# Two graph layers on one core: sums over seen edges go to layer 2's accumulators through DRAM; products of the list use five PSUM banks, additions three bunches behind

## The chip, the cores and the metric

The kernel runs on one core of a Trainium2 chip. The core has five engines with queues of their own: PE (TensorE, matmuls; PEld is its loading of weights), DVE (VectorE), ACT (ScalarE), POOL (GpSimd) and SP (SyncE, which here only issues DMAs). Each works through its instructions in order and waits on semaphores where an instruction needs another engine's or a DMA's result. The metric is device microseconds (us) of one execution, and the median of several runs is compared.

## The reference

A relational graph network of two layers over N = 12,500 nodes of 128 features and 200,000 edges, sorted by their target node. An edge's relation is the greatest of ten of its attributes. In each layer a node takes, for each of ten relations, the mean of its neighbours' features, multiplies it with that relation's matrix, and adds its own features times a root matrix and a bias. The first layer ends in a relu; behind the second come the residual and a layer norm.

```python
def _rgcn_layer(x, src, dst, edge_type, w_rel, root, bias):
    seg = dst * NUM_REL + edge_type
    sums = jax.ops.segment_sum(x[src], seg, num_segments=N * NUM_REL)
    cnt = jax.ops.segment_sum(jnp.ones(seg.shape, x.dtype), seg, num_segments=N * NUM_REL)
    mean = (sums / jnp.maximum(cnt, 1.0)[:, None]).reshape(N, NUM_REL, -1)
    return jnp.einsum('nrd,rdo->no', mean, w_rel) + x @ root + bias
...
edge_type = jnp.argmax(msg[:, NODE_EMB_DIM:-NODE_EMB_DIM], axis=1).astype(jnp.int32)
h = jax.nn.relu(_rgcn_layer(x, src, dst, edge_type, w_rel1, root1, b1))
return _rgcn_layer(h, src, dst, edge_type, w_rel2, root2, b2)      # then _layernorm(x + ...)
```

## The kernel before

**Tiles of edges.** The edges lie in 1,563 tiles of 128. For a tile GpSimd gathers the 128 source rows from DRAM with one indirect DMA (`gathered`, L751) into a buffer `g`; DVE makes a one-hot matrix `oh` of the edges' (relation, node) places (`ones`, L765 in layer 1 and L768 for the list of layer 2); ACT multiplies it with the edges' weights, one over the count (`weighted`, L757); PE multiplies both into a PSUM bank `zp` (L978 in layer 1, L1480 in layer 2); and DVE adds `zp` to the accumulators (`sum_into`, L792) at a place that it reads from a register. In the profile each of these float matmuls counts as two records.

**Accumulators.** `cc` holds two rings in SBUF, one for each layer, of 10 relations x (1,024 nodes + 120 columns beyond the end). The nodes go through a ring in blocks, mostly of 256, so that a lap has four. When a block has all its edges, `folded` (at the start of a lap, L729) adds what lies beyond the end; `projected` (L739, ten matmuls with the relations' matrices, and L742 one for the root) makes the block's output; and the place is cleared by ACT (`cleared`, L722) in two halves for the next lap. The place of an addition is known only as a range of nodes when the program is built. A range that lies across the end of a lap is declared as the whole ring (`offsets`), so that an addition there is ordered behind everything that is still under way in the ring.

**Layer 1** (`layer_1`) walks over all 1,563 tiles. The first 166 gather rows of x (512 B). The other 1,397 gather rows of 1 KB, x and h side by side, from tables in which the h of finished nodes has been written: an edge whose source is finished when the walk comes by is a *seen* edge, and its h row goes to layer 2's ring (ring 1) with the same one-hot, in the same addition (`ALL`). When a block k is done, `finish` issues its projection, and sets for some tiles later (`todo.at`, where u is four tiles): the activation and transposes (`rows_out`), the stores of h by SP (`rows_kept`), `second`, which projects ring 1 with layer 2's matrices and adds root 2 x h, `second_kept`, which adds the bias and stores the result to `T2` in DRAM on SP's queue, and the clears of both rings. `second` and its clears stand for blocks of seen edges (`both`).

**Layer 2** (`layer_2`) has the edges that were not seen. It gathers from `hD`, the h rows in DRAM: first 166 tiles as they were, in the meantime DVE and PE bring the unseen edges together into a list (`brought_together`), then 695 tiles of that list. Two walks share the rings: walk 0 (the low nodes) sums into ring 1, walk 1 into ring 0. The work is cut into bunches, each as many products as one PSUM bank holds. A bunch's one-hots are made four bunches ahead (`AH`) and its additions stand two bunches behind (`BE`); `zp` has three banks (`ps_y`), one more is `ps_m`'s, for the making of the list. There are seven gather buffers `g` of eight tiles and six one-hot buffers (`OB`). A list tile may be wider than 48 places and is then multiplied in column pieces, each with a one-hot table of its own (`tables[(c, WZ)]`). When a block is done, `finish` projects it, adds `T2` through an identity matmul (L742), and sets `turn` (ACT, transposes), `norm` (`normed`, L700 to L710, then the store of the output) and two `cleared` at 8u and 12u.

**Order.** Nothing is left to a planner: each engine's order is that in which the program emits its instructions, and the due times above set it. A queue that waits holds all that stands behind it.

Of the kernel before, what the change touches and what calls it, by code (L numbers as in the profile page):

```python
# [32 lines left out]
OB = 6  # L33
# [31 lines left out]
def rgcn_resnorm_kernel(ctx: ExitStack, tc: tile.TileContext, x, src, dst, attr, w_rel1, root1, b1,  # L65
# [145 lines left out]
    T2 = dram.tile([C, N], F32, name="T2")  # L211
# [426 lines left out]
    def rows_in(k):  # L638

        last = "e" if k == len(ranges[-1]) - 1 else ""  # L640
        xb = fin.tile([P, len(block(k)[2]) if last else 4, C], F32, name="xb" + last)
        rows_dma(xb, x, k, False)
        return xb

    def features_in(k, l, xb):

        n0, n, subs = block(k)
        last = "e" if k == len(ranges[-1]) - 1 else ""
        fT = fin.tile([P, (len(subs) if last else 4) * P], F32, name="fT" + last)
# [17 lines left out]
    def shifted(po, k, l):  # L667

        n = block(k)[1]
        tail = {NBLK - 1: "e", NBLK - 2: "d"}.get(k, "")  # L670
        a = fin.tile([P, P if tail else YB], F32, name="a" + tail)
        nc.scalar.activation(a[:, :n], po[:, :n], AF.Identity if l else AF.Relu, bias=bsb[l])  # L672
        return a
# [19 lines left out]
    def normed(k, xb, pr):  # L693

        v = fin.tile([P, 4, C], F32, name="v")
# [12 lines left out]
        o = fin.tile([P, 4, C], F32, name="o")  # L708
        for t, h in subs:
            nc.vector.tensor_scalar(o[:h, t, :], v[:h, t, :], mv[:h, t, 0:1], rstd[:h, t:t + 1],  # L710
                                    op0=ALU.subtract, op1=ALU.mult)
        rows_dma(o, out, k, True)
# [19 lines left out]
    def projected(k, l, last, po=None, more=True, ring=None):  # L732

        n0, n, _ = block(k)
        o = n0 % RN
        if po is None:
            po = ps_f.tile([P, YB], F32, name="pf")
        for r in range(NREL if more else 0):
            nc.tensor.matmul(po[:, :n], wsb[l][:, r, :], cc[:, l if ring is None else ring, r, o:o + n],  # L739
                             start=(r == 0), stop=False)  # L740
        w, f = last
        nc.tensor.matmul(po[:, :n], w, f[:, :n], start=not more, stop=True)  # L742
        return po
# [15 lines left out]
    def ones(keys, cols, n, w):  # L759

        oh = dpool.tile([P, YB], F32, name="oh")
        m = NREL * w
        o = oh[:, :n * m]
        if w == WN:
            nc.vector.tensor_tensor(o.rearrange("p (t m) -> p t m", m=m), cols[:, None, :m].to_broadcast([P, n, m]),  # L765
                                    keys[:, :, None].to_broadcast([P, n, m]), op=ALU.is_equal)
        else:
            nc.vector.tensor_tensor(o.rearrange("p (t r n) -> p t r n", r=NREL, n=w),  # L768
                                    cols[:, None, :, :w].to_broadcast([P, n, NREL, w]),
                                    keys[:, :, None, None].to_broadcast([P, n, NREL, w]), op=ALU.is_equal)  # L770
        return oh
# [60 lines left out]
    def layer_1():  # L832
# [6 lines left out]
        def finish(k, t):  # L839
# [8 lines left out]
            po = [projected(k, 0, (rsb[0], fTs[k]))]  # L848
# [4 lines left out]
            def rows_out(_):  # L853
                a = po.pop()
                a = fin_a.setdefault(k, shifted(a, k, 0))
                pr = ps_f.tile([P, 4, C], F32, name="pf")
                n0, n, subs = block(k)
# [33 lines left out]
            if k < NBLK - 1:  # L891
                todo.at(t + (9 if k >= NBLK - 3 else 3) * u, second)
                todo.at(t + (9 if k >= NBLK - 3 else 4) * u, second_kept)
            else:
                todo.run(t)
                todo.run(END)
                todo.at(t, second)
                todo.at(t, second_kept)
# [4 lines left out]
            if k + 1 < NBLK - 1:  # L903
# [10 lines left out]
                def turned_kept(t):  # L914
                    n0, n, subs = block(k + 1)
                    pt = po.pop()
                    fTs[k + 1] = fin.tile([P, 4 * P], F32, name="fT")
# [6 lines left out]
        fin_a = {}  # L924
# [117 lines left out]
    ps_m = fast.enter_context(tc.tile_pool(name="ps_m", bufs=1, space=PSUM))  # L1042
    ps_y = fast.enter_context(tc.tile_pool(name="ps_y", bufs=3, space=PSUM))
    idxB = comp.tile([P, NT2], I32, name="idxB")
# [13 lines left out]
    def brought_together(ready, first):  # L1058
# [15 lines left out]
        for to, a, o in ((Si, src, 0), (A[:, P:], CN, 0), (K, KD, L)):  # L1074
# [3 lines left out]
            if whole < NR:  # L1078
                nc.sync.dma_start(to[whole:NR, :real], bass.AP(a.tensor, a.offset + o + (NT - RT) * P, [[ER, 1], [1, real]]))
        tri, wide = flat[:, at:at + P], flat[:, at + P:at + P + NREL * WZ].rearrange("p (r n) -> p r n", n=WZ)  # L1080
        assert at + P + NREL * WZ <= NREL * RW
        yield 1
        nc.vector.tensor_tensor(wide, spread[:, :, None].to_broadcast([P, NREL, WZ]),
                                columns[:, None, :WZ].to_broadcast([P, NREL, WZ]), op=ALU.add)
# [85 lines left out]
        for c in range(0, WMAX, WZ):  # L1170
            w = min(WZ, WMAX - c)
            t = mask[:, c * NREL:(c + w) * NREL].bitcast(F32).rearrange("p (r n) -> p r n", n=w)
            nc.vector.tensor_scalar(t, wide[:, :, :w], float(c), None, op0=ALU.add)
            tables[c, WZ] = t
        assert WMAX * NREL <= ER
# [5 lines left out]
        def put(i, c):  # L1181
# [5 lines left out]
            o = WMAX * NREL + i * (EW // P)  # L1187
# [101 lines left out]
    def layer_2():  # L1289
# [90 lines left out]
        def fetched(k):  # L1380
# [4 lines left out]
            if k != partial:  # L1385
                assert k != final or partial in ended
                xbs[k] = (comp if tail else fin).tile([P, 4, C], F32, name="xb" + tail)
                rows_dma(xbs[k], x, k, False)
            fTs[k] = (comp if tail else fin).tile([P, 4 * P], F32, name="fT" + tail)
            nc.sync.dma_start(fTs[k][:, :n], T2[:, n0:n0 + n])  # L1390

        def finish(k, i):
# [8 lines left out]
            po = [projected(k, 1, (ident, fTs[k]), ring=ring)]  # L1401
# [10 lines left out]
            def turn(_):  # L1412
                a = fin.tile([P, YB], F32, name="a")
                nc.scalar.activation(a[:, :n], po.pop()[:, :n], AF.Copy)
                if k == partial:
                    nc.sync.dma_start(T2[:, n0:n0 + n], a[:, :n])
                    fetched(following[0])
                    return
                pr = ps_f.tile([P, 4, C], F32, name="pf")
# [25 lines left out]
        AH, BE = 4, 2  # L1445
# [5 lines left out]
        for p in range(-AH, NB + BE):  # L1451
            if p + AH < NB:
# [3 lines left out]
                ohs[p + AH] = ones(keys[:, t0:t0 + n], tables[(c, WZ) if second else WN], n, w)  # L1456
# [6 lines left out]
            if p < 0:  # L1463
                continue
            if p < NB:
# [23 lines left out]
            q = p - BE  # L1489
            if q >= 0:  # L1490
                l, second, t0, n, w, c, whole = bunches[q]
                assert not l or "ring" in ready
                for j in range(n):
                    t = t0 + j
                    if (second, t) not in offs:
# [4 lines left out]
                        else:  # L1500
                            m = min(GB2, T0 - t)
                            if t % CT == 0:
                                row = rows_.tile([1, CT], I32, name="row")
                                nc.scalar.dma_start(row, b_i[t // CT:t // CT + 1, :])
                            vals = offsets(row[:, t % CT:t % CT + m], t, m, bounds)
# [184 lines left out]
```

## Time and profile before

| | us |
|---|---|
| median of the runs (3112.14 to 3119.51) | 3114.19 |
| the profiled execution | 3108.35 |
| its span, first to last instruction | 3106.5 |
| PE busy | 2368.2 |
| PEld busy | 1949.5 |
| DVE busy | 2031.1 |
| ACT busy | 1301.6 |
| POOL busy | 2295.8 |

The mean granted TensorE clock was 0.84 of full speed. Layer 1's gathers run from 4 to 1,958 us, layer 2's from 1,969 to 3,052 us. DMA moved 370.97 MB. A row of the costliest groups has a line, an engine, an operation, out<-in, a count, then busy time and the mean of one in ns, then the idle time of the engine ahead of them and what ended most of it. A row of the waits has the waiting line, what it waited for, microseconds in total, times, and the longest. A row of a timeline has the start, the duration, the instruction, and in brackets the idle time before it and what ended that.

### The profile page before, as it was taken

Reading aid. Unit: us, or ns where it says so; the run is one execution under the profiler, and the core shown is the slowest. Engines: PE = TensorE matmul, PEld = TensorE weight load, DVE = VectorE, ACT = ScalarE, POOL = GpSimd, SP = SyncE. Lnnn points to the kernel's source line nnn. Section 1 sums busy time; section 2 is a strip of 40 time slices with the busy share of each in tenths; the row PEclk is TensorE's granted clock in tenths of the full one; section 3 lists DMA queues with packets and bytes.
Section 4 is the critical chain, followed back from the end, with each engine's and each line's share of the span. In section 5 each row is a group of like instructions: output and inputs, shape, how many; then the busy total and the mean of one; then the engine's idle time right before and its main releaser. Section 6 shows DMA issues by size and latency. Waiting matters only on the chain.

```text
span 3106.5 us, 42362 instructions
## 1 busy us (share of the span) xinstructions
PE 2368.2 (76%) x11861; PEld 1949.5 (63%) x11861; DVE 2031.1 (65%) x5465; ACT 1301.6 (42%) x3177; POOL 2295.8 (74%) x2436
## 2 busy tenths in 40 slices
PE   2768787888787878787878788546467777777887
PEld 1556677777776767676767677545445555555665
DVE  6764657665656767655646464597776676777766
ACT  3533443433333434333433333332434455555643
POOL 7777777777777777777777777677777777777772
PEclk8768888888888889888888888767788888998988
DMA  6874444444545454545454444322222222222221
GB/s 191 270 216 143 141 145 141 140 146 122 161 122 162 124 157 129 159 122 160 125 158 127 128 121 118 95 59 62 64 67 68 72 73 74 72 73 73 79 73 43
DMA packets 265199, 370.97 MB, mean 119 GB/s; under 512 B 51232, under 2 KB 197189, under 8 KB 264958
## 3 DMA queue, kind: packets, MB, share of 16 engines
q0 software_dynamic: 99920, 250.57, 29.4%
q1 hardware_dynamic: 111347, 91.97, 9.4%
q10 hardware_dynamic: 53691, 25.62, 2.8%
q8 instruction: 102, 1.67, 0.2%
q14 instruction: 139, 1.14, 0.1%
HBM read 322.86 MB, written 57.89 MB: 123 GB/s over the span
## 4 chain that ended last, share of the span: by engine, by line
PE 30%; POOL 22%; issue 19%; DVE 14%; DMA 10%; ACT 2%; DVEq 1%; ACTq 0%; POOLq 0%; SPq 0%
POOL g L751 22%; PE pf L739 13%; DMA g<-XH,idxE 9%; PE zp L978 8%; PE zp L1480 6%; DVE cc L792 5%; DVE oh L768 2%; PE pf L742 1%; DVE cc L1158 1%; DVEq L777 1%; ACT cc L722 1%; ACT oh L757 1%; DVE oh L765 1%; DVE st L703 1%; DVE go L1146 1%
## 5 line engine op out<-in xcount | busy, mean ns | idle before, releaser
L751 POOL DMA_INDIRECT g<-XH,idxE x1397 | 1321.2, 946 | 425.6 <-issue 384.8
L792 DVE TENSOR_TENSOR cc<-cc,zp 128x240 f32 (+13 forms) x2500 | 959.8, 384 | 777.8 <-PE zp L978 388.2
L978 PE MATMUL zp<-oh,g 128*128 128x120 f32 x5920 | 983.2, 318 | 370.5 <-DMA g<-XH,idxE 206.8
L978 PEld LDWEIGHTS zp<-oh,g 128*128 128x128 f32 x5920 | 866.5, 222 | 487.2 <-issue 184.8
L751 POOL DMA_INDIRECT g<-hD,idxB x695 | 657.3, 946 | 215.9 <-issue 195.3
L739 PE MATMUL pf<-cc,w 128*128 128x256 f32 (+4 forms) x3000 | 732.1, 405 | 18.9 <-DVE cc L792 15.1
L1480 PE MATMUL zp<-oh,g 128*128 128x120 f32 (+23 forms) x1874 | 507.3, 415 | 284.4 <-DVE cc L792 156.4
L739 PEld LDWEIGHTS pf<-cc,w 128*128 128x128 f32 x3000 | 610.4, 215 | 121.1 <-DVE cc L792 22.5
L1480 PEld LDWEIGHTS zp<-oh,g 128*128 128x128 f32 x1874 | 338.9, 227 | 430.9 <-issue 271.0
L757 ACT ACTIVATE oh<-oh,wE 128x120 f32<-128x120 f32 x1729 | 530.9, 383 | 186.0 <-DVE oh L765 139.4
L757 ACT ACTIVATE oh<-oh,wB 128x150 f32<-128x150 f32 (+23 forms) x771 | 339.1, 482 | 296.5 <-DVE oh L768 269.4
L722 ACT ACTIVATE cc<-zero 128x1280 f32<-128x1280 f32 (+3 forms) x274 | 336.6, 1231 | 85.3 <-DVE cc L792 81.5
L768 DVE TENSOR_TENSOR oh<-go,keyB 128x480 f32<-128x480 f32 (+20 forms) x476 | 260.3, 547 | 115.1 <-PE zp L1480 113.6
L672 ACT ACTIVATE a<-pf,b 128x256 f32<-128x256 f32 (+1 forms) x50 | 23.3, 465 | 580.6 <-PE pf L742 578.9
L765 DVE TENSOR_TENSOR oh<-bank,keyE 128x480 f32<-128x480 f32 x391 | 253.0, 647 | 0.0
L751 POOL DMA_INDIRECT g<-hD,idxE x166 | 158.8, 957 | 61.7 <-issue 46.0
L751 POOL DMA_INDIRECT g<-in_x_dram,idxE x166 | 156.9, 945 | 52.2 <-issue 47.9
L883 ACT ACTIVATE v<-pf,b 128x256 f32<-128x256 f32 (+2 forms) x52 | 23.9, 459 | 361.4 <-PE pf L742 333.2
L548 DVE TENSOR_TENSOR eqb<-bank,kh 128x1344 bf16<-128x1344 f32 (+2 forms) x65 | 100.4, 1549 | 2.4 <-PE pf L559 2.0
L557 PE MATMUL pf<-eqb,identb 128*128 128x512 bf16 (+2 forms) x130 | 58.9, 453 | 12.4 <-DVE eqb L548 12.4
L559 PE MATMUL pf<-eqb,identb 128*128 128x512 bf16 (+2 forms) x130 | 58.5, 450 | 0.0
L706 ACT ACTIVATE rstd<-mv,eps 128x2 f32<-128x2 f32 (+5 forms) x54 | 15.9, 295 | 83.8 <-DVE mv L704 83.3
(235 smaller groups left out, 1097.8 us busy)
## 6 DMA issues: line engine op xcount, KB each, us to landing
m<-in_edge_attr_dram SPq DMA_DIRECT2D x48, 672.0 KB
g<-XH,idxE POOLq DMA_INDIRECT x1397
XH<-in_x_dram ACTq DMA_DIRECT2D x24, 512.0 KB
XH<-zero ACTq DMA_DIRECT2D x24, 512.0 KB
XH<-hb SPq DMA_DIRECT2D x87, 128.0 KB
g<-hD,idxB POOLq DMA_INDIRECT x695
xb<-in_x_dram SPq DMA_DIRECT2D x72, 128.0 KB
out_dram<-o SPq DMA_DIRECT2D x47, 128.0 KB
```

The lines of the kernel that those rows point to most:

```text
L548: nc.vector.tensor_tensor(eq[:p], kpP[:p, None, :R].to_broadcast([p, DB, R]), fore, op=ALU.is_equal)
L557: nc.tensor.matmul(pc[:p], identb[:p, :p], eq[:p, k:k + 4, L:], start=(d + k == 1), stop=False)
L559: nc.tensor.matmul(pc[:p], identb[:p, :p], back, start=False, stop=(d + k + 3 == L))
L722: nc.scalar.activation(cc[:, l, h * H:(h + 1) * H, o:o + n], zero[:, None, :n].to_broadcast([P, H, n]), AF.Copy)
L739: nc.tensor.matmul(po[:, :n], wsb[l][:, r, :], cc[:, l if ring is None else ring, r, o:o + n], start=(r == 0), stop=False)
L751: nc.gpsimd.indirect_dma_start(out=g[:, j * C:(j + n) * C], out_offset=None, in_=table, in_offset=bass.IndirectOffsetOnAxis(ap=idx, axis=0))
L757: nc.scalar.activation(s, s, AF.Copy, scale=w)
L765: nc.vector.tensor_tensor(o.rearrange("p (t m) -> p t m", m=m), cols[:, None, :m].to_broadcast([P, n, m]), keys[:, :, None].to_broadcast([ ...
L768: nc.vector.tensor_tensor(o.rearrange("p (t r n) -> p t r n", r=NREL, n=w), cols[:, None, :, :w].to_broadcast([P, n, NREL, w]), keys[:, :, ...
L792: nc.vector.tensor_tensor(s, s, z, op=ALU.add)
L978: nc.tensor.matmul(zp[:, a + l * KW:a + (l + 1) * KW], g[:, (slot[j] + l) * C:(slot[j] + l + 1) * C], oh[:, j * KW:(j + 1) * KW], start=Tr ...
L1480: nc.tensor.matmul(zp[:, j * m:(j + 1) * m], gt[:, b * C:(b + 1) * C], oh[:, j * m:(j + 1) * m], start=True, stop=True)
```

## The change

Layer 1 no longer projects ring 1. A finished block's h, transposed, goes to `hT` in DRAM, and its ten sums of seen edges go from ring 1 to a new tensor `S2` [128, 10, 12500] in DRAM, 1.31 MB for a block of 256; ring 1 is cleared as before. Layer 2 does not clear a place behind a projection: `sums_back` loads into it the sums of the nodes that come a lap later, and the projection adds root 2 x h from `hT` where it added `T2`. `T2` is left for the one block which both walks share (`partial`, `final`). There are 48 stores and 45 loads of S2; the clears go from 274 to 186.

When the making of the list is over, `ps_m` is closed and its space holds two more banks for products and one one-hot table; from the list's first bunch on, products take turns in five banks and additions stand three bunches behind (for the first 166 tiles two, as before). OB goes from 6 to 7. One-hots of the later column pieces come from that one table, with the piece's first column added in the same instruction, where a table had been made for each piece. The rows of offsets for layer 2's first tiles are loaded at its start on SP's queue. Some tiles hold three sub-blocks of 128 where they held four.

```diff
-OB = 6
+OB = 7
...
+    S2 = dram.tile([C, NREL, N], F32, name="S2")
+    T2 = dram.tile([C, YB], F32, name="T2")
...
-    def projected(k, l, last, po=None, more=True, ring=None):
+    def projected(k, l, ring, lasts):
...
+        for i, (w, f, a, b) in enumerate(lasts):
+            nc.tensor.matmul(po[:, a:b], w, f[:, :b - a], start=False, stop=(i == len(lasts) - 1))
...
+            if c:
+                assert n == 1
+                nc.vector.scalar_tensor_tensor(to[:, 0], a[:, 0], float(c), b[:, 0], op0=ALU.add, op1=ALU.is_equal)
...
-            def second(_):
-                po.append(projected(k, 1, (rsb[1], fin_a.pop(k)), more=both))
-
-            def second_kept(_):
-                n0, n, _ = block(k)
-                p2 = po.pop()
-                t2 = fin.tile([P, YB], F32, name="v")
-                nc.scalar.activation(t2[:, :n], p2[:, :n], AF.Identity, bias=bsb[1])
-                nc.sync.dma_start(T2[:, n0:n0 + n], t2[:, :n])
+            hs = []
+
+            def sums_kept(_):
+                nc.sync.dma_start(hT[:, n0:n0 + n], hs.pop()[:, :n])
+                if both:
+                    o = n0 % RN
+                    nc.sync.dma_start(S2[:, :, n0:n0 + n], cc[:, 1, :, o:o + n])
...
+            todo.at(t + 3 * u, sums_kept)
...
+        def sums_back(l, a, b):
+
+            ring = 1 - l
+            while a < min(b, (shared[1], N)[l]):
+                e = min(b, (shared[1], N)[l], a // RN * RN + RN)
+                nc.sync.dma_start(cc[:, ring, :, a % RN:a % RN + e - a], S2[:, :, a:e])
+                a = e
...
-            po = [projected(k, 1, (ident, fTs[k]), ring=ring)]
+            lasts = [] if k == partial else [(rsb[1], fTs[k], 0, n)]
+            if k == final:
+                lasts.insert(0, (ident, fTs[NB2], n - ranges[-1][partial][1], n))
+            po = [projected(k, 1, ring, lasts)]
...
             if clear[k]:
-                todo.at(min(i + 8 * u, by), lambda i: cleared(ring, k, 0))
-                todo.at(min(i + 12 * u, by), lambda i: cleared(ring, k, 1))
+                todo.at(min(i + 2 * u, by), lambda i: sums_back(1 - ring, n0 + RN, n0 + n + RN))
...
-        AH, BE = 4, 2
+        AH, BE = 4, 3
+        plain = sum(not b[1] for b in bunches)
+        rowP = comp.tile([1, -(-T0 // CT) * CT], I32, name="rowP")
+        for c in range(-(-T0 // CT)):
+            nc.sync.dma_start(rowP[:, c * CT:(c + 1) * CT], b_i[c:c + 1, :])
...
+            if p == plain - AH:
+                assert wanted[0] in ready
+                masking.close()
+                ps_n = fast.enter_context(tc.tile_pool(name="ps_n", bufs=1, space=PSUM))
+                tables[WZ] = ps_n.tile([P, NREL, WZ], F32, name="wide")
...
-                zp = zps[p] = ps_y.tile([P, YB], F32, name="zp")
+                if p % 5 > 2 and five:
+                    zp = ps_n.tile([P, YB], F32, name=f"zq{p % 5}")
+                else:
+                    zp = ps_y.tile([P, YB], F32, name="zp")
+                zps[p] = zp
...
-            q = p - BE
-            if q >= 0:
+            if "ring" in ready and "sums" not in ready:
+                ready.add("sums")
+                sums_back(1, shared[1], shared[0] + RN)
+            q = p - (BE if five else BE - 1)
+            if q in zps:
```

More of the change, by code (lines that the diff above doesn't have):

```diff
@@ L640, in rows_in @@
         last = "e" if k == len(ranges[-1]) - 1 else ""
-        xb = fin.tile([P, len(block(k)[2]) if last else 4, C], F32, name="xb" + last)
+        xb = fin.tile([P, len(block(k)[2]) if last else 3, C], F32, name="xb" + last)
         rows_dma(xb, x, k, False)
@@ L648, in features_in @@
         last = "e" if k == len(ranges[-1]) - 1 else ""
-        fT = fin.tile([P, (len(subs) if last else 4) * P], F32, name="fT" + last)
+        fT = fin.tile([P, (len(subs) if last else 3) * P], F32, name="fT" + last)
         if l:
@@ L730, in folded @@
         nc.vector.memset(e, 0.0)
-    def projected(k, l, last, po=None, more=True, ring=None):
+    def projected(k, l, ring, lasts):
         n0, n, _ = block(k)
         o = n0 % RN
[L736 to L742, printed above, removed]
+        po = ps_f.tile([P, YB], F32, name="pf")
+        for r in range(NREL):
+            nc.tensor.matmul(po[:, :n], wsb[l][:, r, :], cc[:, ring, r, o:o + n],
+                             start=(r == 0), stop=(r == NREL - 1 and not lasts))
+        for i, (w, f, a, b) in enumerate(lasts):
+            nc.tensor.matmul(po[:, a:b], w, f[:, :b - a], start=False, stop=(i == len(lasts) - 1))
         return po
@@ L1169, in brought_together @@
         yield 1
[L1170 to L1175, printed above, removed]
         n = -(-NT2 // P)
@@ L1455, in layer_2 @@
                 assert not second or {t0 // P, (t0 + n - 1) // P} <= ready
-                ohs[p + AH] = ones(keys[:, t0:t0 + n], tables[(c, WZ) if second else WN], n, w)
+                ohs[p + AH] = ones(keys[:, t0:t0 + n], tables[WZ if second else WN], n, w, c)
             if 0 <= p + AH - 1 < NB:
@@ L1464, in layer_2 @@
                 continue
+            five = p >= plain
             if p < NB:
@@ L1501, in layer_2 @@
                             m = min(GB2, T0 - t)
[L1502 to L1505, printed above, removed]
+                            vals = offsets(rowP[:, t:t + m], t, m, bounds)
                         offs = {k: v for k, v in offs.items() if k[0] and (k[1] >= UX) != l}
```

73 lines of the change are left out of this document (38 added, 35 removed).

## The prediction

> **What bounds the kernel now.** I read the page's costliest groups first, then a table of windows, GpSimd's timeline, and the waits.
>
> ```profile
> span 3106.5 us, 42362 instructions
> ...
> L751 POOL DMA_INDIRECT g<-XH,idxE x1397 | 1321.2, 946 | 425.6 <-issue 384.8
> ...
> L751 POOL DMA_INDIRECT g<-hD,idxB x695 | 657.3, 946 | 215.9 <-issue 195.3
> L739 PE MATMUL pf<-cc,w 128*128 128x256 f32 (+4 forms) x3000 | 732.1, 405 | 18.9 <-DVE cc L792 15.1
> ```
>
> A gather costs GpSimd 946 ns and some 0.30 us before the next: 425.6/1397 in layer 1, 215.9/695 in layer 2. No other engine is that regular. The windows (PE, PEld, DVE, ACT, POOL busy, granted clock, DMA share, GB/s) show 159 to 161 GpSimd instructions per 200 us, and 81 in the 100 us where the DMA engines are 0.89 busy; DMA load has not slowed the gathers.
>
> ```profile
> 100.00:200.00 100.00, 71.29 (x343) 58.39 (x342) 62.89 (x177) 48.54 (x136) 75.61 (x81) 0.76 0.89 272
> 2400.00:2600.00 200.00, 156.18 (x585) 105.81 (x584) 136.04 (x367) 104.31 (x210) 149.91 (x159) 0.88 0.28 73
> 2600.00:2800.00 200.00, 150.71 (x639) 111.08 (x637) 145.06 (x399) 111.96 (x241) 149.66 (x159) 0.93 0.28 74
> 2800.00:3000.00 200.00, 166.21 (x662) 124.49 (x662) 149.66 (x403) 114.10 (x237) 151.25 (x161) 0.90 0.28 73
> ```
>
> So 2424 gathers (166 + 1397 + 166 + 695) at about 1.25 us are about 3028 us of the span. GpSimd's own timeline shows what is left: one pause at the change of layers, two short ones, and an end 54.6 us before the span's.
>
> ```profile
> 1957.12 0.95 POOL L751 DMA_INDIRECT g<-XH,idxE  x1 [0.30 <-issue]
> 1969.45 0.94 POOL L751 DMA_INDIRECT g<-hD,idxE  x1 [11.38 <-PE pf L742]
> ...
> 2482.81 0.94 POOL L751 DMA_INDIRECT g<-hD,idxB  x1 [2.01 <-PE zp L1480]
> ...
> 2493.04 0.94 POOL L751 DMA_INDIRECT g<-hD,idxB  x1 [0.55 <-PE zp L1480]
> ...
> 3050.91 0.94 POOL L751 DMA_INDIRECT g<-hD,idxB  x1 [0.30 <-issue]
> ```
>
> The two short pauses wait for a product: the gather buffers are full. How far the consumers are behind, by windows of the gathers' line and of the products' line (two records a product):
>
> ```profile
> 1960.00:2325.00 365.00, 269.31 (x283) 0.72 0.26 67
> 1960.00:2625.00 665.00, 494.82 (x522) 0.79 0.27 69
> ```
> ```profile
> 1960.00:2325.00 365.00, 114.05 (x497) 89.96 (x497) 0.72 0.26 67
> 1960.00:2625.00 665.00, 266.31 (x992) 176.75 (x992) 0.79 0.27 69
> 3052.00:3107.00 55.00, 18.01 (x64) 13.82 (x64) 0.88 0.14 32
> ```
>
> The first 166 tiles take 332 records; the page's 1874 leave 1542, or 771 products for 695 list tiles: 1.11 a tile, since wide tiles are cut. At 2325 that is 166 + (497-332)/2/1.11 = 240 tiles against 283 gathers, 43 behind (54 us). At 2625 it is 463 against 522, 59 behind: the cap, since seven buffers hold 56. After 3052, 64 records or 29 tiles remain, 36 us of gathers. So in layer 2 the consumers, PE and DVE in turn, are late, and their debt is paid in the tail. In layer 1 it is the other way round (waits from 260 to 1950):
>
> ```profile
> PE zp L978 <- DMA g<-XH,idxE: 196.9, 278, 3.7
> ...
> DVE cc L792 <- PE pf L739: 102.5, 11, 11.6
> ```
>
> PE there waits 278 times for gathers; it is not late.
>
> **The change, part by part.** *Layer 1's second projections go.* 48 blocks x 20 records x 405 ns = 389 us if taken at the page's mean, which mixes cold and wide forms; either way it is PE time beside gathers that PE waits for. I cost it at nothing. Its cover is the GpSimd pace and seven gather buffers, which hold 28 of the tables' 1 KB rows' gathers: 35 us.
>
> *The stores of S2.* 48 of 256 columns x 10 x 128 x 4 B = 1.31 MB, on SP's queue; in total 11,476 columns, 58.8 MB. The page's queue row and the nearest single transfers price them:
>
> ```profile
> q1 hardware_dynamic: 111347, 91.97, 9.4%
> ```
> ```profile
> L825 ACTq DMA_DIRECT2D XH<-in_x_dram x26: 497/1227/2567, 44.1 to 200.3; - x26
> ```
> ```profile
> 1967.04 0.33 SPq L634 DMA_DIRECT2D hD<-hb  x1
> ...
> 1976.37 0.83 SPq L1077 DMA_DIRECT2D cc<-in_src_dram  x2
> ...
> 1983.91 1.68 DVE L1095 SCALAR_TENSOR_TENSOR cc<-cc,seen_below,go 127x1408 bf16<-127x1408 int32 x1 [13.43 <-DMA cc<-in_src_dram]
> ```
>
> 9.4% of 16 x 3106.5 us for 91.97 MB is 50.8 engine-us per MB; 1.31 MB over 16 engines is 4.2 us. To it I add 1.2 us of issue (the median above) and 2.0 to landing (a small store issued by 1967.37 releases the gather at 1969.45): 7.4 us. The upper bound is 12 us: 7.5 us passed from 1976.37 to 1983.91 for loads of about half that size. In layer 1 store and landing delay the clears of ring 1 by some 10 us; a lap is four blocks, so the next use is far, save where a wrapped range is declared over the whole ring and an addition must wait for the store, about once a lap, some 5 us, 11 times. The gather buffers cover that. The hD stores stand ahead of the last S2 stores on SP's queue, so the pause of 11.38 us stays; between -2 and +5 us I take 0. If the cover were gone, 11 x 5 = 55 us would show.
>
> *The loads of S2 in layer 2.* 45 DMAs instead of 88 half-ring clears on ScalarE, issued soon after the block's projection. Behind each on SP stand the fetches of x and hT and the output stores, needed ten gathers later or not at all. What waits is DVE: an addition with a wrapped range has to wait for the load. Counting DVE's instructions in the changed order at their mean times here, in 12 of 45 places less than 11 us of other DVE work stands between the projection and such an addition (2.5, 4.6, 2.1, 9.0, 4.2, 2.3, 2.1, about 5, 4.2, about 5, about 8, and 0.4 for the last, some 44 us ahead of the last gather). Each stalls DVE 4.6 us (the projection) + 7.4 - that work: about 75 us in all, 47 of them from 2310 to 2610, 27 later. Between 5 us (bytes and little else) and 12 us a load, the 12 stalls are 46 to 130 us. I take 7.4, as its parts are rows of the same kind of queue. By the Trainium skill, DMA: Bandwidth & Descriptors, section "Anatomy of one DMA", such a DMA costs 2.0 us + bytes/436 GB/s, an estimate of 5.0 us; the sum by that is 29 us of stall less. No run here shows it; the load at 1983.91 was slower than that rule gives.
>
> *Five banks, three bunches behind, one more one-hot buffer.* From 2250 to 2700 and from 2700 to 3050 the waits they act on are:
>
> ```profile
> PE zp L1480 <- DVE cc L792: 69.0, 36, 5.9
> DVE oh L768 <- PE zp L1480: 63.3, 24, 5.4
> ...
> DVE cc L792 <- PE pf L739: 21.4, 4, 6.6
> ...
> DVE cc L792 <- ACT cc L722: 7.7, 9, 1.2
> ```
> ```profile
> DVE oh L768 <- PE zp L1480: 43.8, 19, 4.6
> ...
> DVE cc L792 <- PE pf L739: 14.2, 3, 5.8
> ...
> DVE cc L792 <- ACT cc L722: 4.3, 6, 0.9
> ```
>
> During a projection (20 records, 4.6 us) DVE today can only go two bunches on, and then stands. With a bunch more on either side I take half of 63.3 and 43.8 as gone, between none and all. The waits for projection and clear (29.1 and 18.5) are inside the load's stall now.
>
> *Rest.* The offsets of the first tiles come early instead of a DMA per 128; its wait (rows: 14.8 us, 2 times, longest 9.4) loses the 9.4 in layer 2. Fused one-hots, 73, cost as the others. The bias in the turn, smaller tiles: nothing, beside GpSimd.
>
> ```profile
> DVE cc L792 <- DMA row<-b_i: 14.8, 2, 9.4
> ```
>
> *The tail* is on the path.
>
> ```profile
> 3084.51 4.88 PE L739 MATMUL pf<-cc,w 128*128 128x280 f32 x20
> ...
> 3089.70 0.58 PE L1480 MATMUL zp<-oh,g 128*128 128x250 f32 x2
> ...
> 3090.80 4.64 PE L739 MATMUL pf<-cc,w 128*128 128x260 f32 x20
> 3095.28 0.60 PE L742 MATMUL pf<-fTe,ident 128*128 128x260 f32 x2
> ...
> 3096.42 0.55 PE L1421 MATMUL pf<-ident,a 128*128 128x128 f32 x3 [0.54 <-ACT a L1414]
> ...
> 3099.27 0.84 DVE L710 TENSOR_SCALAR o<-v,mv,rstd 128x128 f32<-128x128 f32 x3
> ```
>
> Now 16.2 us pass from the last product (3090.28) to the end, because the 280 projection runs before it. In the changed order the last product comes first, then 280 projection 5.4, turn 0.5, transposes 0.6, its norm on DVE 3.1 (as from 3097.01 to 3100.1), five additions 2.1, 260 projection with the partial block 5.7, and the same end 10.6; with 0.5 of handover, 28.5 us. That is 12.3 us lost.
>
> **The sum.** The last gather ends at 3051.85 - 1.96 (the pauses' excess over 0.30) = 3049.9. Lag at 2325: 54 - 9.4 = 45, less 5 that I estimate for the projections between 2200 and 2325: 40 us. To 2610: stalls before 63.3 + 29.1 = 92, after 47 + 32 = 79; I call it level. From 2625 the debt falls 22 us as now (58 to 36), and 62.3 - (27 + 22) = 13 more: 40 - 35 = 5 to 6 us at the last product. 3049.9 + 6 + 28.5 = 3084.4 of span. The profiled execution took 3108.35, 1.85 over its span, and the median is 5.84 above that: 3092.
>
> **Rivals.** *(B) The consumers catch up only in part:* lag 12 to 20, as when the banks give a quarter; 3100 to 3107. *(E) It doesn't matter:* the gathers set the pace, PE's saving is hidden, and the tail's 12.3 us take what the lag gives: lag 22 to 34: 3092 - 6 + lag is 3108 to 3120. For it: the steady 159 to 161. *(C) Slower by the additions' waits:* DVE's stall at each wrapped load replaces what the banks give, and the lag ends as it is now, 38: 3092 + 32 = 3124. It decides as soon as loads take about 10 us (12 x 2.6 = 31 us more). Against it: DMA share falls to 0.28 in layer 2, so loads are alone. *(D) Loads of 12 us:* 55 us more stall, the lag stays at the cap of 58 to the end and GpSimd pauses: 3135 to 3160. *(F) Layer 1's stores slow the gathers:* share 0.47 to about 0.6, under the 0.89 which did not; 55 us, 3147; against it the first window.
>
> **How the numbers follow.** Catch-up (A), 3084 to 3100: 0.42. B: 0.14. E: 0.12. C, 3120 to 3132: 0.20. D and F: 0.12. The predicted time is A's. Range 3083 to 3132: it leaves out D and F, and 0.05 of A's floor and C's end; A alone would be 3084 to 3100. 0.2% is 6 us, about what the three runs (3112 to 3119) can tell from none: faster under 3108, A and B, 0.56; same, 3108 to 3120, 0.12; slower, C, D, F, 0.32.
>
> **What would show it.** Right: 159 to 161 gathers per 200 us, no pauses at 2480; after the last gather under ten tiles; a last product some 28 us ahead of the end; DVE waits for cc from S2 about 12 times at 5 to 10 us. Wrong: over 25 tiles left after the last gather; GpSimd waiting for products (then loads are longer than 10 us); gathers below 155 per 200 us in layer 1.

## The result, and the profile after

The changed kernel took 3097.15 us (median of five runs, 3090.85 to 3100.65); the kernel before, in five runs beside it, 3113.22 us. The ratio is 0.9943, with a 95% interval from 0.9927 to 0.996: faster by 0.6%. The forecast was 3092, in a range of 3083 to 3132. The profiled execution of the changed kernel took 3097.15 us, 1.95 over its span.

The page of the changed kernel, its span and the costliest groups:

```profile
span 3095.2 us, 40345 instructions
...
L751 POOL DMA_INDIRECT g<-XH,idxE x1397 | 1321.7, 946 | 429.2 <-issue 390.9
...
L739 PE MATMUL pf<-cc,w 128*128 128x256 f32 (+5 forms) x2040 | 521.3, 418 | 69.6 <-DVE cc L797 44.6
```

The gathers are what they were. 960 records of the projections' matmuls are gone. Its windows (PE, PEld, DVE, ACT, POOL busy, granted clock, DMA share, GB/s), first the bulk of layer 1, then three of layer 2:

```profile
260.00:1950.00 1690.00, 1259.10 (x6787) 1091.43 (x6786) 1031.63 (x2757) 636.96 (x1646) 1275.45 (x1349) 0.78 0.57 171
```
```profile
2400.00:2600.00 200.00, 152.69 (x589) 106.65 (x587) 132.50 (x362) 82.38 (x189) 151.06 (x161) 0.89 0.50 144
2600.00:2800.00 200.00, 156.23 (x658) 116.18 (x658) 150.98 (x416) 94.76 (x230) 151.25 (x160) 0.90 0.49 141
2800.00:3000.00 200.00, 165.12 (x710) 130.15 (x710) 158.49 (x430) 99.42 (x232) 150.92 (x160) 0.93 0.47 135
```

GpSimd still issues 160 or 161 gathers per 200 us with the DMA engines at 0.47 to 0.50 where they were at 0.28. TensorE runs 710 records from 2800 to 3000 where it ran 662: the consumers go faster than the gathers and catch up. How far they are behind, by the gathers' line and the products' line:

```profile
1960.00:2325.00 365.00, 268.24 (x283) 0.70 0.40 109
1960.00:2625.00 665.00, 494.92 (x523) 0.78 0.43 120
```
```profile
1960.00:2325.00 365.00, 116.51 (x504) 93.76 (x505) 0.70 0.40 109
1960.00:2625.00 665.00, 259.09 (x996) 179.22 (x997) 0.78 0.43 120
3052.50:3096.00 43.50, 7.49 (x32) 5.76 (x32) 0.83 0.11 21
```

By the count used in the prediction, 283 - (166 + 172/2/1.11) = 40 tiles at 2325 (43 before) and 523 - 465 = 58 at 2625 (59 before), where the buffers are full in either kernel; after the last gather 32 records are left where there were 64. GpSimd's timeline has a wait that it had not before, in layer 1 (with a smaller one of 1.14 us for a product at 1618.29), and the pause between the layers as it was:

```profile
1177.28 0.94 POOL L751 DMA_INDIRECT g<-XH,idxE  x1 [2.98 <-DMA XH<-hb]
...
1973.19 0.94 POOL L751 DMA_INDIRECT g<-hD,idxE  x1 [11.10 <-DMA hD<-hb]
...
3051.54 0.94 POOL L751 DMA_INDIRECT g<-hD,idxB  x1 [0.30 <-issue]
```

In layer 2 the kernel before paused four times for products. The prediction shows the first two; the others are these:

```profile
2685.34 0.94 POOL L751 DMA_INDIRECT g<-hD,idxB  x1 [2.29 <-PE zp L1480]
...
2695.52 0.94 POOL L751 DMA_INDIRECT g<-hD,idxB  x1 [0.50 <-PE zp L1480]
```

In the changed kernel one is left, 0.92 us at 2945.83. VectorE's waits from 2250 to 3050:

```profile
DVE cc L797 <- DMA cc<-S: 54.4, 10, 10.0
DVE cc L797 <- PE pf L739: 36.1, 7, 6.3
...
DVE oh L775 <- PE zp L1504: 20.8, 9, 3.4
DVE oh L775 <- PE zq L1504: 19.8, 6, 5.1
DVE oh L773 <- PE zp L1504: 14.9, 7, 2.7
...
DVE oh L773 <- PE zq L1504: 2.5, 1, 2.5
```

The wait for products that have to free a one-hot buffer (the four `oh` rows) falls from 107.1 (63.3 + 43.8) to 58.0 us. New is the wait for the loads of S2, ten times and 54.4 us. The wait for projections has stayed: 36.1 us for 35.6 (21.4 + 14.2). In layer 1, from 260 to 1950, VectorE's additions now wait for the stores of S2:

```profile
DVE cc L797 <- DMA S<-cc: 85.1, 11, 9.9
...
DVE cc L797 <- PE pf L739: 10.8, 1, 10.8
```

Eleven waits for stores have come for the eleven for projections that the kernel before had there (102.5 us; one is left), and the pace of the gathers hides them as it hid those. The end of the timeline:

```profile
3060.93 2.53 PE L1504 MATMUL zp<-oh,g 128*128 128x250 f32 x10 [1.93 <-DVE cc L797]
...
3064.93 4.99 PE L739 MATMUL pf<-cc,w 128*128 128x280 f32 x20 [1.47 <-DVE cc L797]
...
3073.88 0.84 DVE L711 TENSOR_SCALAR o<-v,mv,rstd 128x128 f32<-128x128 f32 x3
...
3074.65 2.31 DVE L797 TENSOR_TENSOR cc<-cc,zp 128x250 f32 x5
3077.02 6.76 PE L739 MATMUL pf<-cc,w 128*128 128x260 f32 x20 [5.44 <-DVE cc L797]
```

The last product ends at 3063.46, 11.0 us behind the last gather's end at 3052.48 (38.4 before). From there to the end 31.8 us pass (16.2 before): the norm of the block of 280 stands on VectorE ahead of the last five additions, and the last projection behind these.

So the ledger, in us: layer 1's last gather ends 4.0 later (1962.1 for 1958.1), layer 2's gathers take 3.1 less from first to last (1079.3 for 1082.4), the pause 0.3 less, the lag 27.4 less, the tail 15.6 more. The span is 11.3 shorter. Of layer 1's 4.0, the waits at 1177.28 and 1618.29 are 3.5 beyond the usual 0.30 each.

### The profile page after: what moved, and what is told of

Same layout as the page of the kernel before. It is cut to its first block, busy times and chain, and to the rows that moved or that the text cites. A ratio compares the mean times of both kernels' runs of the same rounds, so it can differ in the third digit from the quotient of the medians.

```text
span 3095.2 us, 40345 instructions
## 1 busy us (share of the span) xinstructions
PE 2212.9 (71%) x10797; PEld 1826.2 (59%) x10797; DVE 2025.7 (65%) x5462; ACT 1192.9 (39%) x3037; POOL 2296.5 (74%) x2436
## 3 DMA queue, kind: packets, MB, share of 16 engines
q14 instruction: 139, 1.14, 0.1%
## 4 chain that ended last, share of the span: by engine, by line
PE 26%; DVE 20%; POOL 17%; issue 16%; DMA 16%; ACT 2%; DVEq 2%; ACTq 0%; SPq 0%; POOLq 0%
POOL g L751 17%; PE pf L739 11%; DMA g<-XH,idxE 10%; PE zp L976 9%; DVE cc L797 8%; DVE oh L775 3%; DMA cc<-S 2%; PE zp L1504 2%; DMA S<-cc 2%; DVE oh L765 1%; PE zq L1504 1%; DVEq L782 1%; PE pf L742 1%; DVE cc L1155 1%; DVE st L704 1%
## 5 line engine op out<-in xcount | busy, mean ns | idle before, releaser
L976 PE MATMUL zp<-oh,g 128*128 128x120 f32 x5920 | 1062.0, 336 | 516.1 <-DMA g<-XH,idxE 357.0
L797 DVE TENSOR_TENSOR cc<-cc,zp 128x240 f32 (+11 forms) x2193 | 839.9, 383 | 744.3 <-PE zp L976 422.1
L739 PE MATMUL pf<-cc,w 128*128 128x256 f32 (+5 forms) x2040 | 521.3, 418 | 69.6 <-DVE cc L797 44.6
L739 PEld LDWEIGHTS pf<-cc,w 128*128 128x128 f32 x2040 | 429.3, 220 | 157.2 <-DVE cc L797 58.1
L1504 PE MATMUL zp<-oh,g 128*128 128x120 f32 (+20 forms) x1260 | 324.5, 402 | 166.6 <-DVE cc L797 98.1
L723 ACT ACTIVATE cc<-zero 128x1280 f32<-128x1280 f32 (+1 forms) x186 | 227.3, 1226 | 321.2 <-DVE cc L797 162.8
L775 DVE TENSOR_TENSOR oh<-wide,keyB 128x480 f32<-128x480 f32 (+17 forms) x400 | 229.2, 573 | 44.3 <-PE zq L1504 23.4
L1504 PE MATMUL zq<-oh,g 128*128 128x160 f32 (+21 forms) x614 | 172.1, 412 | 62.1 <-issue 28.8
L1504 PEld LDWEIGHTS zq<-oh,g 128*128 128x128 f32 x614 | 110.7, 214 | 109.5 <-issue 77.7
L797 DVE TENSOR_TENSOR cc<-cc,zq 128x160 f32 (+21 forms) x307 | 119.5, 389 | 57.5 <-PE pf L739 24.0
```

The costliest lines, as they stand in the source:

```text
L723: nc.scalar.activation(cc[:, l, h * H:(h + 1) * H, o:o + n], zero[:, None, :n].to_broadcast([P, H, n]), AF.Copy)
L739: nc.tensor.matmul(po[:, :n], wsb[l][:, r, :], cc[:, ring, r, o:o + n], start=(r == 0), stop=(r == NREL - 1 and not lasts))
L775: nc.vector.tensor_tensor(to, a, b, op=ALU.is_equal)
L797: nc.vector.tensor_tensor(s, s, z, op=ALU.add)
L976: nc.tensor.matmul(zp[:, a + l * KW:a + (l + 1) * KW], g[:, (slot[j] + l) * C:(slot[j] + l + 1) * C], oh[:, j * KW:(j + 1) * KW], start=Tr ...
L1504: nc.tensor.matmul(zp[:, j * m:(j + 1) * m], gt[:, b * C:(b + 1) * C], oh[:, j * m:(j + 1) * m], start=True, stop=True)
```

## The experiments

Two theories were to be told apart: that the slack (five banks, three bunches behind, seven one-hot buffers) lets the consumers catch up while the sums through DRAM are neutral, and that the sums pay, with their 88 clears and 960 records less.

**The sums alone**

```diff
-OB = 7
+OB = 6
...
-        AH, BE = 4, 3
+        AH, BE = 4, 2
...
-                if p % 5 > 2 and five:
-                    zp = ps_n.tile([P, YB], F32, name=f"zq{p % 5}")
-                else:
-                    zp = ps_y.tile([P, YB], F32, name="zp")
+                zp = ps_y.tile([P, YB], F32, name="zp")
...
-            q = p - (BE if five else BE - 1)
+            q = p - BE
```

> The sums through DRAM alone: three product banks, additions two bunches behind, six one-hot buffers, the rest as in the changed kernel. My theory (the slack of banks and bunches pays, the sums through DRAM are neutral in layer 2): the consumers stay at the cap of the gather buffers past 2600 us and end 35 to 45 us late, the tail is short again (about 17 us): 3104 to 3118 us. Rival (the sums pay: fewer projections and clears): the lag ends near 11 us as in the changed kernel and the tail is short: 3080 to 3088 us.

Measured: 3164.83 us (3164.72 to 3171.61), 1.0168 of the kernel before, from 1.0154 to 1.0182. Neither theory's time: the sums alone are a loss of 50 us. Two of GpSimd's rows, and VectorE's waits from 2250 to 3080:

```profile
2492.55 0.94 POOL L751 DMA_INDIRECT g<-hD,idxB  x1 [9.55 <-PE zp L1501]
...
2712.53 0.94 POOL L751 DMA_INDIRECT g<-hD,idxB  x1 [9.48 <-PE zp L1501]
```
```profile
DVE oh L775 <- PE zp L1501: 98.9, 49, 5.3
DVE cc L797 <- DMA cc<-S: 44.8, 9, 6.4
DVE cc L797 <- PE pf L739: 34.9, 7, 6.9
...
DVE oh L773 <- PE zp L1501: 15.2, 4, 5.2
```

The wait for the loads comes on top of the others: 114.1 us for products in the way and 34.9 for projections, where the kernel before has 107.1 (63.3 + 43.8) and 35.6 from 2250 to 3050. The gather buffers stay full, so that GpSimd pauses (its gathers of layer 2 take 1111.7 us for 1082.4), and the last product ends 63.0 us behind the last gather for 38.4. These two are 54 us more than in the kernel before; the wait for loads, less 12.0 us of waits for clears that go, and 7.0 more for products are 40 of them. The other 14 are not accounted for. One candidate is the clock: from 2250 to 3050 it was 0.84 where it had been 0.89, and a record of a product took 450 ns in the mean for 428; how much of that lay on the path no run shows. In layer 1, without the second projections and with the stores, the last gather ends at 1958.9 for 1958.1.

**The banks alone.** The kernel before, with the five banks, three bunches behind, seven one-hot buffers and one table: `second`, `second_kept`, `T2` and the clears as they were.

```diff
-            def sums_kept(_):
-                nc.sync.dma_start(hT[:, n0:n0 + n], hs.pop()[:, :n])
-                if both:
...
+            def second(_):
+                po.append(projected(k, 1, 1, [(rsb[1], hs.pop(), 0, n)], more=both))
...
-                todo.at(min(i + 2 * u, by), lambda i: sums_back(1 - ring, n0 + RN, n0 + n + RN))
+                todo.at(min(i + 8 * u, by), lambda i: cleared(ring, k, 0))
+                todo.at(min(i + 12 * u, by), lambda i: cleared(ring, k, 1))
```

> The banks alone: five product banks, additions three bunches behind and seven one-hot buffers as in the changed kernel, but layer 1 projects ring 1, T2 carries the result and ScalarE clears in layer 2 as before. My theory: lag at the end 5 to 15 us, tail 29 to 32 us as in the changed kernel: 3088 to 3102 us. Rival (the sums pay, the banks don't): lag 35 us and more with the long tail: 3118 to 3130 us.

Measured: 3092.56 us (3084.98 to 3093.43), 0.9928 of before, from 0.9914 to 0.9941. Banks, bunches and buffers together carry the whole gain; the interval overlaps that of the changed kernel, so that the sums on top of them are neutral or a small loss. What each of the three gives, and the single table with the early offsets, was not tried apart. The profiled execution took 3084.98, 7 us under the other four (3092.03 to 3093.43), so the rows show the fastest case. VectorE's waits from 2250 to 3050 show no load, and TensorE's show gathers that it waits for:

```profile
DVE cc L796 <- PE pf L738: 48.7, 9, 10.1
DVE oh L774 <- PE zp L1494: 30.2, 17, 4.7
DVE oh L774 <- PE zq L1494: 29.9, 12, 5.8
...
DVE oh L772 <- PE zp L1494: 15.7, 8, 4.1
...
DVE cc L796 <- ACT cc L722: 9.9, 13, 1.0
...
DVE oh L772 <- PE zq L1494: 1.4, 1, 1.4
```
```profile
PE zp L1494 <- DMA g<-hD,idxB: 19.4, 29, 1.7
```

The four `oh` rows are 77.2 us, less than the 107.1 of before but more than the changed kernel's 58.0; TensorE's waits for a free bank (`zp` and `zq` behind L796, from 2250 to 3050) are 42.8 us, where they were 102.3 before and are 58.0 in the changed kernel. TensorE waits 29 times for gathers ahead of `zp`, where it waited 4 times before, a sign that it has caught up; the lag at the last product is 5.2 us, the tail 30.5. Layer 1's last gather ends at 1958.4, with all second projections in it: these cost nothing at this pace.

**Clears in the place of the loads**

```diff
-                todo.at(min(i + 2 * u, by), lambda i: sums_back(1 - ring, n0 + RN, n0 + n + RN))
+                todo.at(min(i + 8 * u, by), lambda i: cleared(ring, k, 0))
+                todo.at(min(i + 12 * u, by), lambda i: cleared(ring, k, 1))
```

> The changed kernel with ScalarE's two clears at 8u and 12u in the place of each load behind a projection; it leaves out the seen edges' sums that those loads bring. My theory: the waits for loads (some 50 us of VectorE after 2300) go, those for projections and clears come back (some 30 to 45 us): 3088 to 3098 us. Rival (the loads are what keeps the consumers late): the lag falls to the floor well ahead of the end, 3080 to 3087 us.

This kernel leaves out the sums that those loads bring. Measured: 3097.45 us (3088.27 to 3098.77), 0.9944 of before, from 0.9931 to 0.9958: the changed kernel's time. The profiled execution is the one of 3088.27; there the lag at the last product is 5.2 us for 11.0. The loads are worth some 6 us by the profiles and nothing by the medians; what the other four runs spent 9 us on is not in any trace.

**The tail.** The last bunches are added two behind, and the last block's projection is issued ahead of the turn and norm of the block before it.

```diff
-            todo.run(END)
+            if k != final:
+                todo.run(END)
...
             po = [projected(k, 1, ring, lasts)]
+            if k == final:
+                todo.run(END)
...
-            q = p - (BE if five else BE - 1)
-            if q in zps:
+            for q in range(summed, p - (BE if five and p < NB - 2 else BE - 1) + 1):
+                summed = q + 1
+                if q in zps:
...
-            todo.run(i)
+            if not due or due[0][1] != final:
+                todo.run(i)
```

> The changed kernel with another order at the very end: the last bunches are added two behind, and the last block's projection stands ahead of the turn and the norm of the block before it. My theory (the tail's length is that order): from the last product to the end 20 to 23 us for 31.8: 3084 to 3090 us. Rival (the tail is set by the slower clock and the stores): 3093 to 3100 us.

Measured: 3095.31 us (3094.01 to 3100.2), 0.9941 of before, from 0.9928 to 0.9955. As a time it is the rival's, as a tail the theory's:

```profile
3067.44 4.98 PE L739 MATMUL pf<-cc,w 128*128 128x280 f32 x20 [0.72 <-DVE cc L797]
...
3073.36 0.42 DVE L797 TENSOR_TENSOR cc<-cc,zp 128x250 f32 x1 [3.97 <-PE zp L1508]
3073.83 4.65 PE L739 MATMUL pf<-cc,w 128*128 128x260 f32 x20 [0.51 <-DVE cc L797]
```

From the last product to the end 20.1 us pass for 31.8, and the last projection takes 4.65 us for 6.76: TensorE has not been idle ahead of it, and its granted clock was 1.00 from 3073 to 3079, where in the changed kernel it was 0.69 from 3077 to 3084. But the last product now stands behind the 280 projection, which adds to the lag (14.8 for 11.0), and in this execution the last gather came 6.0 us later: GpSimd's gathers took 949.0 ns in the mean for 946.8, over 2424 of them 5 us. From the last gather's end to the end it is 34.9 us for 42.7, so 7.8 of the 11.7 us are left.

**At a slower pace.** The remaining runs came on three other chips, where every kernel, the one before too, took about 29% longer; they are read only against runs on the same chip. There the kernel before took 4044, 3999 and 4000 us. Four kernels ran on the first chip: the sums alone with clears for the loads, which leaves out the sums that the loads bring (once on each of the other two chips as well), the changed kernel with each load issued twice, the changed kernel with layer 1's second projections issued again, unread, and the banks alone with the tail's order (on the other two as well).

```diff
+                for _ in range(2):
+                    nc.sync.dma_start(cc[:, ring, :, a % RN:a % RN + e - a], S2[:, :, a:e])
```
```diff
+            def second(_):
+                projected(k, 1, 1, [(rsb[1], hs[0], 0, n)])
...
+            if k < NBLK - 1 and both:
+                todo.at(t + 3 * u, second)
```

> The sums alone (three banks, two behind, six one-hot buffers) with ScalarE's clears in the place of the loads behind projections; it leaves out the seen edges' sums that those loads bring. Theory (the waits for loads, on top of those for projections, are what made the sums alone slower by 50 us): 3105 to 3122 us, lag at the end 30 to 45 us. Rival (the loss is elsewhere: the stores in layer 1, the fused one-hots, root 2 in layer 2): 3145 to 3168 us.

> The changed kernel with each load of S2 issued twice in a row. Theory (about ten loads are waited for in full): each of these waits grows by 4.2 us (bytes) to 7.4 us (all of it), 42 to 74 us; the lag at the end, 11 us now, grows to 40 and more and GpSimd pauses at full buffers: 3122 to 3160 us. Rival (loads hide behind the gather pace when there are five banks): 3090 to 3102 us.

> The changed kernel with layer 1's second projections issued again on TensorE, their result not used. Theory (layer 1 waits for gathers, the projections are beside them): 3090 to 3102 us, the granted clock in layer 1 back from 0.78 to about 0.85. Rival (their removal saves time): 3110 us and more, with GpSimd pauses in layer 1.

> The banks alone (T2 and clears as before) with the tail's order of the experiment on the tail. Theory (nothing but the gathers, a floor lag of 2 to 5 us and the tail is left): from the last gather's end to the end 23 to 28 us for 35.7: 3080 to 3086 us. Rival (with the consumers at the floor the last projections wait for the last gather whatever their order): 3089 to 3094 us.

On the first of these chips, the last four columns from one profiled execution each, in us:

```
                            median  of before (95%)           layer 1's last  layer 2's  lag at last  last product
                                                              gather's end    gathers    product      to the end
sums, 3 banks, clears      4067.76  1.0050 (1.0032 to 1.0067)         2565.7     1398.1         58.6          18.1
changed, loads twice       4110.08  1.0148 (1.0120 to 1.0176)         2565.9     1417.2         66.4          32.0
changed, idle projections  4065.09  1.0054 (1.0035 to 1.0073)         2592.1     1356.1         63.0          31.8
banks alone, new tail      4012.00  0.9917 (0.9894 to 0.9940)         2548.6     1339.9         66.1          19.2
```

VectorE's waits for loads, with loads twice from 2900 to 4010, and with idle projections, whose layer 2 is the changed kernel's, from 2900 to 3980:

```profile
DVE cc L797 <- DMA cc<-S: 96.5, 10, 12.2
```
```profile
DVE cc L797 <- DMA cc<-S: 36.3, 8, 7.3
```

At this pace the consumers are late to the end in all four: from 2900 to 3900 GpSimd waits for products 213, 152, 143 and 229 us (loads twice, idle projections, banks, sums). So what VectorE loses layer 2 loses. Doubling the loads adds 60 us to that wait and 61 to layer 2's gathers: a load that is waited for is on the path. The new tail takes 19.2 us for 32. With the second projections in both, the stores of S2 cost layer 1 43.5 us (2592.1 for 2548.6), and with the stores in both, the projections cost it 26 (2592.1 for 2565.7 and 2565.9): at this pace layer 1 does not cover them, as it does at the other. These are single executions; stores without projections ended layer 1 17 us later than projections without stores here, and 30 and 39 us later on the other two chips. The rows of GpSimd say where the stores act: in layer 1, to 2560, it waits for writes of h into the tables 194 to 216 us in the five runs with stores, and 152 to 178 us in the three without. The granted clock from 300 to 2500 was 0.72 in the two without second projections, and 0.75 and 0.77 with them.

> The sums alone with clears in the place of the loads behind projections, as in e9_three_banks_clears, on a chip at full pace: the leaving out is the same. Theory (the waits for loads are the loss of the sums alone): 3105 to 3122 us, lag at the end 30 to 45 us. Rival (the loss is elsewhere): 3145 to 3168 us.

> The banks alone with the tail's new order, as in e7_banks_tail, on a chip at full pace. Theory: from the last gather's end to the end 23 to 28 us for 35.7: 3080 to 3086 us. Rival (at the floor the last projections wait for the last gather whatever their order): 3089 to 3094 us.

> The sums alone with clears in the place of the loads behind projections; the leaving out is that of e9_three_banks_clears. At full pace (before at 3114): 3105 to 3122 us if the waits for loads are the loss of the sums alone, 3145 to 3168 us if it is elsewhere. At the slow pace (before at 4000 and more): 1.003 to 1.010 of before, as in the two runs of it so far.

> The banks alone with the tail's new order. At full pace: 3080 to 3086 us if the tail's order is worth some 10 us there, 3089 to 3094 us if the last projections wait for the last gather whatever their order. At the slow pace: 0.990 to 0.995 of before, as in the two runs of it so far.

Measured: the sums with clears 1.0079 (1.0058 to 1.0099) and 1.0095 (1.0066 to 1.0123); the banks with the new tail 0.9934 (0.9917 to 0.9952) and 0.9921 (0.9895 to 0.9947). Both at the slow pace, on either chip. The time of either at full pace was not seen. By parts, the best version would be the banks alone with the new tail; that it would take some 3081 to 3085 us is an estimate, 3092.56 less the 11.7 us of tail or less the 7.8 that tail and lag together gave. Whether the loads alone make the 50 us of the sums alone was therefore not tried at the pace where it arose; what stands for it is the ledger of waits above, with 14 us open.

## Why the prediction was right, and where its terms were off

**The direction and its cause** were right: the gathers set the pace, the consumers were late in layer 2 alone, and the slack let them catch up. The wait that was to fall by half fell from 107.1 to 58.0 us, a little less than half. The banks alone show the slack as the cause; that this one wait carries it they don't show, since there it fell to 77.2 us only, and TensorE's waits for a bank fell more. The case of catch-up is the one that came by its time, but not in full: 32 records, or 14 tiles, were left after the last gather, where the sign was under ten.

**The sums through DRAM** I had as neutral in layer 2, and one step of that was wrong: "The waits for projection and clear ... are inside the load's stall now." The waits for projections stayed in full (36.1 us). With the loads' 54.4 VectorE stands 90.5 us where I had 75 for both. The 75 was a slip: the twelve places as I listed them add up to 95 (12 x 12.0 less 49.4), which would have put the forecast some 20 us later, at 3112. The loads are ten that are waited for, where I counted 12. One of them, by SP's row and VectorE's:

```profile
2483.59 0.53 SPq L1394 DMA_DIRECT2D cc<-S  x1
```
```profile
2490.07 0.57 DVE L797 TENSOR_TENSOR cc<-cc,zq 128x400 f32 x1 [4.59 <-DMA cc<-S]
```

From issue to the waiting addition 6.5 us pass; in all nine of 1.31 MB it is 6.4 to 7.7, 6.6 in the middle, where I had 7.4, and the tenth, of 0.88 MB, took 5.4. By the Trainium skill (DMA: Bandwidth & Descriptors, "Anatomy of one DMA") 2.0 us plus the bytes at 436 GB/s gives an estimate of 5.0 us, below all nine; the section states this for DMAs on GpSimd's path, and I had applied it to SP's. Rival C's mechanism, in which the loads' waits eat the gain, is seen in the sums alone: without the banks they were 50 us slower than the kernel before, a size that I had in none of the theories for them.

**Layer 1's projections** at nothing: right at full pace. **The stores of S2** at nothing: off by the 4.0 us by which layer 1's last gather came later. Additions do wait for them eleven times, as I had counted, though 7.7 us each for my 5, and the gather buffers cover that. I had looked at who waits for the store, not at who stands behind it on SP's queue. The gather at 1177.28 waits for a write of h rows into the tables; SP's queue ahead of it:

```profile
1168.28 0.53 SPq L887 DMA_DIRECT2D S<-cc  x1
1168.86 8.95 SPq L635 DMA_DIRECT2D XH<-hb  x2
```

A store of 1.31 MB stands between two such writes; which of them the gather waited for the rows don't say. In the sums alone a gather at this place waits 0.57 us, so it varies from one execution to the next, and at full pace the store as its cause is only argued. At the slow pace the longer waits for these writes in all runs with stores speak for it.

**The lag**: at 2325 I had 40 us, and it was 40 tiles or 49 us, only 5 less than before; "level" to 2610 was wrong too, since by 2625 it stood at the cap (58 tiles) as in the kernel before. It fell later and faster than I had: 58 tiles are 72 us, so it fell 61 us from there to the last product, where I had 35, and ended at 11.0 us for my 5 to 6. My 35 held a slip of units: "22 us as now (58 to 36)" takes 36 us from 58 tiles, and in us the kernel before fell some 38 (74 to 36). So the lag came out nearly right by luck: a start 9 us higher than I had, a rise of some 23 that I had as level, and a fall of 61 that I had as 35, nearly cancel.

**The tail**: 28.5 forecast, 31.8 measured. The order was read rightly; the last projection took 6.76 us, not 4.64, after 5.4 us without work for TensorE, and the 280 projection began 1.5 us late behind additions.

**The sum**: span 3084.4 forecast and 3095.2 measured; 2.6 us of the difference are the last gather's, 5.0 the lag's, 3.3 the tail's. The last gather's term hid another slip: I had read two of layer 2's four pauses, and without all four it would have been 3047.7, which the banks alone reach (3047.4). My median stood 5.84 us above the profiled execution, as it had before; this time the profiled execution was the median, which hid half of the miss.

## What to carry to other kernels

Where one engine paces a kernel and another is late only in one stage, look for the in-order waits of the late one: here more banks, bunches and buffers were worth 22 us, and 960 matmul records fewer were worth nothing at full pace. A transfer that replaces work on a side engine is not free if an in-order engine has to wait for it; count the waits that come on top, not those that it should replace. And a lag that is worked off leaves the drain's order as the next term: here a norm ahead of five additions on VectorE, and the projections' order, were worth 12 us of the tail in one execution, and 8 with the lag that the new order added.

## What the runs showed of the hardware that I had not expected

TensorE's granted clock from 260 to 1950 fell from 0.85 to 0.78 when it got less to do (1259 us busy for 1392), and its products took 336 ns for 318; where the engine isn't the bound, fewer matmuls bought slower ones. This row of the kernel before stands against that of the changed kernel above:

```profile
260.00:1950.00 1690.00, 1392.41 (x7766) 1209.51 (x7764) 1032.30 (x2760) 653.41 (x1694) 1278.10 (x1353) 0.85 0.47 139
```

In the banks alone, which keep the second projections, it was 0.85 again (1387 us busy). The Trainium skill has a rule for this (TensorE: Matmul & The Clock Gate, "Part 1: The HAM clock gate"): the throttled state is the default and activity releases it; these windows agree, and so does the last projection, 6.76 us after idle time at a clock of 0.69 and 4.65 without at 1.00. Further, chips differ: on some the same program took 29% longer, with the idle time of several engines put down to nothing in the kernel, and there layer 1 no longer covers what it covers at the other pace.
